# Slot attention and a feed-forward layer on one core: keys and gated values transposed by the DMA crossbar, output products between q and v, one burst of quarter-array products

## The chip, the cores and the metric

The kernel runs on one core of a Trainium2 chip. The metric is the device time of one execution in microseconds (us). A median of several executions is given, and beside it the one execution that the profiler recorded.

## The reference

Only the shapes and the data flow matter here. `x` is (2, 2048, 512) in float32.

```python
q, k, v = heads(x @ Wq, 64), heads(x @ Wk, 64), heads(x @ Wv, 128)        # 16 heads
s = clip(heads(x @ Ws, 64), -32, 32)                                      # 64 slots
z = cumlogsumexp(s, time);  p = exp(s - z);  g = exp(z_before - z)
hk = hk * g + k p^T;   ok = q hk           # per head, along time (a scan)
pv = softmax(ok)
hv = hv * g + p v^T;   ov = pv hv          # a second scan
o = rmsnorm(ov) * g_norm * silu(x @ Wg)    # gate, 128 values a head
x = layernorm(x + o @ Wo)
hidden = silu(x @ W1.T) * (x @ W3.T)       # 2048 wide
x = layernorm(x + hadamard(hidden) @ W2.T) # returned
```

The decay is carried by unnormalized exponentials: e = exp(s), a running sum z of e along time, and a division by z at the end. So both scans become masked products inside a chunk and a running state between chunks.

## The kernel before

Everything is float32. Every large product is made by Strassen's method on 2 x 2 blocks: seven block products, numbered 1 to 7, in place of eight. A product k accumulates into one of three PSUM banks, `SUM = {1: c1, 6: c1, 7: c1, 4: c1, 5: c2, 3: c2, 2: c3}`; between two products of one bank a copy of ScalarE (L462, L464) or an addition of VectorE (L467, L755) takes out what is there. A `Unit` holds these three banks; c1 has two buffers, c2 and c3 one each. The right-hand factor of a product is a tile of seven blocks: `b11, b21, b22` and four sums and differences (`right_sums`, L436 to L439).

The attention part runs over 4 groups of 4 heads (`g`) and 16 chunks of 128 positions (`n`): 64 steps. Both rows of the batch are in one step. A step has these parts:

- `load_x` (L477, or L481, L482, L485 in the first group) and `make_x` (L436 to L439, the four sums, first group alone; the finished tile is stored in DRAM, L491).
- `q`: seven products for queries, keys and slot scores (L507; order 1, 2, 5, 6, 7, 3, 4), collected in `t1`.
- `exp_s`: clamp (L515, VectorE), `e2 = exp` (L519), the old running sum added in row 0 (L520, GpSimd), `e = exp` (L521).
- `v`: seven products for values and gate (L533; order 1, then 6, 5, 2, 7, 3, 4), collected in `t2`; `tanh` (L543) and `silu` (L547) make the gate.
- products of a quarter of the array (64 x 64), two heads' halves at a time, after `v(1)`: `scores` (L589), `scores2` (L669, of the step before), `share_of_keys` (L599), `share_of_values` (L681), `slots` (L617), `values` (L692), `state_slots` (L626), `state_values` (L701). The masks `within1` (L593) and `within2` (L675) are VectorE's. This stretch is called the burst below. `running_sum` (L571, two products of the full array with a triangular matrix) stands in the middle of it.
- `reciprocal` in two halves (L582), `softmax` (L634 to L643), `softmax_sum` (L647, and L648 on GpSimd), `gated` (squares L716, products with the gate L718, sum L720, root on GpSimd L722 to L724, product L726).
- transposes: keys by four transposes of TensorE (`k_transposed`, L553, copied out at L555); gated values by eight (`o_transposed`, L743); exponentials and softmax weights by the DMA crossbar. For the crossbar each float32 is split into its two 16-bit halves by GpSimd (`e_split` L560, `r_split` L659), a DMA transposes them (L562, L661) and GpSimd joins them (`e_joined` L566, `r_joined` L665).
- `o`: seven products with Wo (L759), added to the rows (L755); `row_stats` and `normalize` in the last group; `store_rows` (L775), `load_rows` (L734).

`run(new, now, before, old)` writes out by hand the order of these parts for four steps that overlap: `now` is step i, `before` is i-1, `old` is i-2. The engines TensorE, VectorE, ScalarE and GpSimd take instructions in this order. DMAs are all issued from SyncE (SP), whose queue is in order too; where they stand in it the framework decides.

`work_on(1)` to `work_on(4)` let one piece of other work into a step, at four places (called place 1 to 4). In the first group and the beginning of the second it is `up_weights` (sums of blocks of W1 and W3 on VectorE, L784 to L787, L820 to L824; none at place 3); then `down_weights` (a product L867 at one place per step, then butterflies L891, L893); in the last group `block` (sums of the normalized rows) and `rows_transposed` (eight transposes of TensorE). In the first step of a group no piece runs; the sums of the next weights are made there and in the last step of a group (`sums`, L412 to L418).

The feed-forward part follows, with products of 256 columns (L238, L277). The change does not touch it.

The banks: `ps` are two tiles of two banks each; `flat(0)`, `bank(0)` and `bank(1)` lie in the first, scores and slots in the second.

Of the kernel before, what the change touches and what calls it, by code (L numbers as in the profile page):

```python
# [39 lines left out]
def gated_slot_attention_ffn_kernel(  # L40
# [312 lines left out]
    with ExitStack() as att:  # L353
# [87 lines left out]
        class Unit:  # L441


            def __init__(self, width, multiply):
                self.multiply, self.kept = multiply, {}
                for c in ("c1", "c2", "c3"):
                    t = pch.tile([P, 512], F32, name=c, tag=c, bufs=2 if c == "c1" else 1)
                    setattr(self, c, t[:, 0:width])

            def sum(self, k):  # L450
                return getattr(self, SUM[k])

# [16 lines left out]
        class Step:  # L469
# [79 lines left out]

            def k_transposed(self):  # L550

                for i in range(NQ):
                    nc.tensor.transpose(bank(0)[:, i, :], self.t1[:, i, P : 2 * P], ident)  # L553
                self.kr = c1.tile([P, NQ, P], F32, name="kr")
                nc.scalar.copy(self.kr, bank(0))  # L555

            def e_split(self):

                parts = c1.tile([P, 2, NQ * P], U16, name="parts")
                nc.gpsimd.tensor_copy(parts, words(self.e))  # L560
                self.et = c1.tile([P, 2 * NQ, P], U16, name="et")
                nc.sync.dma_start_transpose(out=self.et, in_=parts.rearrange("p h c -> p (h c)"))  # L562

            def e_joined(self):
                self.eT = c1.tile([P, NQ, P], F32, name="eT")
                nc.gpsimd.tensor_copy(words(self.eT), self.et.rearrange("p (h i) t -> p h (i t)", h=2))  # L566

            def running_sum(self):
                p = pch.tile([P, 512], F32, name="running", tag="c1", bufs=2).rearrange("p (i t) -> p i t", t=P)
                for j, h in enumerate(HALVES):  # L570
                    nc.tensor.matmul(p[:, :, h], lhsT=(causal, causal3[:, TH:])[j], rhs=self.e2[:, :, h], start=True, stop=True)  # L571
                z = c1.tile([P, NQ, P], F32, name="z", tag="z")
                nc.scalar.copy(z, p)  # L573
                self.z = z
                if not self.final:
                    for at, h in zip((P - 1, TH - 1), HALVES):
                        nc.sync.dma_start(out=zc[:, :, h], in_=z[at : at + 1, :, h])
                self.iz = c1.tile([P, NQ, P], F32, name="iz")
# [12 lines left out]
            def within1(self):  # L591
                self.a1 = c1.tile([P, 2, NQ, TH], F32, name="a1", tag="r")
                nc.vector.tensor_tensor(self.a1, within_scores[0], within_b, ALU.mult)  # L593

            def share_of_keys(self):

                pk = [pch.tile([P, 512], F32, name="pk", tag=f"c{2 + s}")[:, 0 : NQ * M].rearrange("p (i m) -> p i m", m=M) for s in range(2)]
                for i, j, h, s, t, _ in QUARTERS:
                    nc.tensor.matmul(pk[s][h, i], lhsT=self.kr[t, i, h], rhs=self.e[t, i, h], start=True, stop=True)  # L599

                self.hk = hk[0], hk[1], hk[2]
                hk[0], hk[2] = hk[2], hk[0]
                self.taken_in(self.hk[1], None if self.first else self.hk[0], pk[0])
                if not self.final:
                    self.taken_in(self.hk[2], self.hk[1], pk[1])

# [38 lines left out]
            def softmax_sum(self):  # L645
                self.sm = small.tile([P, NQ, 2], F32, name="sm")
                nc.vector.tensor_reduce(self.sm.rearrange("p q j -> p (q j)"), self.r8, AX.X, ALU.add)  # L647
                nc.gpsimd.tensor_tensor(self.r, self.r, self.iz, ALU.mult)  # L648

# [6 lines left out]
            def r_split(self):  # L656

                parts = c1.tile([P, 2, NQ * P], U16, name="parts_r")
                nc.gpsimd.tensor_copy(parts, words(self.r))  # L659
# [3 lines left out]
            def r_joined(self):  # L663
                self.rT = c1.tile([P, NQ, P], F32, name="rT")
                nc.gpsimd.tensor_copy(words(self.rT), self.rt.rearrange("p (h i) t -> p h (i t)", h=2))  # L665

# [10 lines left out]
            def share_of_values(self):  # L677

                pv = [bank(s) for s in range(2)]
                for i, j, h, s, t, _ in QUARTERS:  # L680
# [5 lines left out]
            def values(self):  # L686

                self.po = [
                    pch.tile([P, 512], F32, name="po", tag=f"c{2 + j}").rearrange("p (i t) -> p i t", t=DV) for j in range(2)
                ]  # L690
                for i, j, h, s, t, o in QUARTERS:
# [14 lines left out]
            def state(self):  # L706
                if not self.final:
                    self.taken_in(hv[0], hv[1], bank(1))

            def gated(self):  # L710
# [4 lines left out]
                for j, to, at in MOVES:  # L715
                    nc.scalar.activation(sq[to, j], self.po[j][at], AF.Square)  # L716
                for j, to, at in MOVES:
                    nc.vector.tensor_tensor(self.gj[to, j], self.po[j][at], self.gj[to, j], ALU.mult)  # L718
                ss = small.tile([P, 2 * NQ], F32, name="ss")
                nc.vector.tensor_reduce(ss, sq.rearrange("p j q d -> p (j q) d"), AX.X, ALU.add)  # L720
                self.state()
                nc.gpsimd.tensor_scalar(ss, ss, 1.0 / DV, 0.0, ALU.mult, ALU.add)  # L722
                nc.gpsimd.tensor_tensor(ss, ss, self.floor.rearrange("p j q -> p (j q)"), ALU.add)
# [13 lines left out]
            def o_transposed(self):  # L737
# [8 lines left out]
                self.ob = c1.tile([P, 7, 2, P], F32, name="ob")  # L746
                right_factor(self.ob, tp)

            def o(self, k):
# [261 lines left out]
        def run(new, now, before, old):  # L1011
# [36 lines left out]

            late = [nw["vg"].sums] if now is steps[0] else []
            if opens:  # L1050
                w["qks"] = nw.pop("qks")
            main("q", 1)
            do(old, "o", 3)
            work_on(1)
            if new is not steps[1]:
                do(new, "load_x")
            main("q", 2)
            do(new, "make_x")
            y["second"] = new is not None and new.g > 0
            work_on(2)  # L1060
            if changes:
                nw["vg"].sums(0, nc.vector)
            main("q", 5)
            do(before, "e_joined")
            work_on(3)
            if changes:
                nw["vg"].sums(1, nc.gpsimd)
            main("q", 6)
            do(old, "o", 6)
            do(before, "r_joined")  # L1070
            if changes:
                nw["vg"].sums(2, nc.vector)
            main("q", 7)
            work_on(4)
            if changes:
                nw["vg"].sums(3, nc.gpsimd)
            main("q", 3)
            main("q", 4)
            do(old, "o", 7)
            if last:  # L1080
                nw["qks"] = load_qks(g + 1)
            if now is steps[-1]:
                wt.append(load_w(0, 0))
                open_x("wqks", OUTER[:3], 3 * P)
            do(now, "exp_s")
            do(now, "e_split")
            do(old, "row_stats", 1)
            for f in late:
                f(0)
            if opens:  # L1090
                w["vg"] = nw.pop("vg")
            main("v", 1)
            more()
            do(before, "load_rows")
            do(now, "k_transposed")
            do(old, "o", 4)
            if o_last:
                nw["o"] = load_o(old.g + 1)

# [5 lines left out]
            do(before, "share_of_values")  # L1107
            do(now, "running_sum")
            do(old, "row_stats", 0)
            do(old, "normalize")  # L1110
            do(old, "store_rows")
            do(now, "reciprocal", 0)
            do(now, "slots")
            do(before, "values")
            do(now, "state_slots")
            do(before, "state_values")
            do(before, "gated")

            for f in late:
# [6 lines left out]
            if o_last:  # L1126
                scale_o()
            do(now, "reciprocal", 1)
            main("v", 2)
# [4 lines left out]
            if last:  # L1134
                nw["qks"].sums(0, nc.gpsimd)
                nw["qks"].sums(1, nc.gpsimd)
            if o_last:
                nw["o"].sums(0, nc.gpsimd)
                nw["o"].sums(1, nc.gpsimd)
            main("v", 7)  # L1140
            do(now, "softmax")
            main("v", 3)
            more()
            do(now, "softmax_sum")
            do(now, "r_split")
            if o_last:
                nw["o"].sums(2)
                nw["o"].sums(3, nc.gpsimd)
            do(before, "o_transposed")
            main("v", 4)  # L1150
            if last:
                nw["vg"] = load_vg(g + 1)
            do(now, "tanh")
            do(now, "squared_sums")
            if before is not None and before.first:
                w["o"] = nw.pop("o")
            do(before, "o", 1)
            do(before, "o", 5)
            more()
# [3 lines left out]
            do(now, "silu")  # L1163
            do(before, "o", 2)
            if now is steps[0]:
# [141 lines left out]
```

## Time and profile before

| what | value |
|---|---|
| median of 3 executions | 3482.67 us (3482.01 to 3483.49) |
| profiled execution, its own time | 3486.9 us |
| its span, first to last instruction | 3485.1 us |
| granted TensorE clock, mean | 0.998 |
| attention, q(1) of the first step to q(1) of the last | 9.7 to 2329.3 us |
| steps 3 to 15 apart (first group) | 35.7 to 36.9 us |
| a step with nothing beside it (1584.0 to 1619.7) | 35.7 us |
| idle of VectorE before L755, in all | 423.5 us |

In the profile PE is TensorE's matmuls, PEld its weight loads, DVE VectorE, ACT ScalarE, POOL GpSimd, SP SyncE, and SPq SyncE's DMA queue. A line of the timeline reads: start in us from the span's start, duration, engine, source line, operation, output <- input, shapes, how often; in brackets the idle time before it and what ended that. Ends of matmuls are modelled and overlap with the next start. A float32 matmul is recorded as two entries. A line of the windows gives the stretch, its length, busy time of each engine, the granted clock of TensorE, the DMA engines' share and GB/s.

### The profile page before, as it was taken

What the parts mean: (1) busy time and instruction counts of PE and PEld (TensorE: products, weight loads), DVE (VectorE), ACT (ScalarE), POOL (GpSimd) and SP (SyncE); (2) the same over time, 40 slices, a digit from 0 to 9 for tenths busy, and PEclk for the clock granted to TensorE, in tenths of its full rate; (3) what the DMA queues carried; (4) which work ended last, traced back from release to release, by engine and by line L of the source; (5) the groups of instructions that cost most, each with busy time, mean ns of one, the idle gap of its engine ahead of it and who ended that gap; (6) DMA issues with size and microseconds to landing.
All of it is one profiled execution on the core that took longest, in us unless ns stands there. A gap on an engine that the chain in (4) does not pass through costs nothing. (4 is left out here: it accounts for less than half of the span.)

```text
span 3485.1 us, 74815 instructions
## 1 busy us (share of the span) xinstructions
PE 3405.6 (98%) x31328; PEld 2664.5 (76%) x31328; DVE 2328.7 (67%) x3812; ACT 912.9 (26%) x1776; POOL 1500.0 (43%) x1389
## 2 busy tenths in 40 slices
PE   8999999999999999999999999998999999999998
PEld 6777776777777777777776777776888888888887
DVE  5777776765657756557656677777667756656756
ACT  2333332333333333333333333332111111111110
POOL 3344344433333543433444334344534634643544
PEclk9999999999999999999999999999999999999999
DMA  6545455433233433323442344467455545444441
GB/s 198 132 131 155 130 144 151 113 87 80 71 76 86 119 105 75 81 74 80 108 112 69 110 130 144 137 190 268 155 187 195 169 162 188 155 157 177 159 135 70
DMA packets 344001, 458.57 MB, mean 132 GB/s; under 512 B 154864, under 2 KB 255600, under 8 KB 342640
## 3 DMA queue, kind: packets, MB, share of 16 engines
q1 hardware_dynamic: 343664, 453.79, 43.7%
q8 instruction: 246, 4.03, 0.5%
q14 instruction: 91, 0.75, 0.1%
HBM read 297.47 MB, written 125.30 MB: 121 GB/s over the span
## 5 line engine op out<-in xcount | busy, mean ns | idle before, releaser
L533 PE MATMUL c<-wvg,xb 128*128 128x512 f32 x1792 | 811.0, 597 | 11.1 <-DVE t L718 7.3
L533 PEld LDWEIGHTS c<-wvg,xb 128*128 128x128 f32 x1792 | 321.8, 189 | 375.0 <-issue 291.7
L507 PE MATMUL c<-xb,wqks 128*128 128x128 f32 x3584 | 550.9, 276 | 26.0 <-DVE t L467 10.6
L507 PEld LDWEIGHTS c<-xb,wqks 128*128 128x128 f32 x3584 | 485.3, 193 | 49.6 <-issue 18.9
L755 DVE TENSOR_TENSOR rows<-c,rows 128x256 f32<-128x256 f32 x448 | 188.6, 422 | 423.5 <-PE c L759 423.0
L219 DVE TENSOR_TENSOR accux<-c,accux 128x512 f32<-128x512 f32 x496 | 341.3, 690 | 182.7 <-PE c L238 166.0
L277 PE MATMUL dc<-w2t,hid 128*128 128x256 f32 x1792 | 455.3, 379 | 2.1 <-DVE res L284 2.1
L238 PE MATMUL c<-wvg,xb 128*128 128x256 f32 x1792 | 433.5, 381 | 5.0 <-DVE accux L219 4.4
L238 PEld LDWEIGHTS c<-wvg,xb 128*128 128x128 f32 x1792 | 340.0, 191 | 56.2 <-DVE accux L219 7.9
L277 PEld LDWEIGHTS dc<-w2t,hid 128*128 128x128 f32 x1792 | 340.2, 190 | 49.5 <-DVE res L284 3.3
L507 PE MATMUL c<-wqks,xb 128*128 128x128 f32 x1792 | 347.9, 276 | 0.0
L238 PE MATMUL c<-wqks,xb 128*128 128x256 f32 x1344 | 326.6, 382 | 6.5 <-DVE accux L219 3.6
L462 ACT COPY kept<-c 128x384 f32<-128x384 f32 (+1 forms) x384 | 203.0, 529 | 426.9 <-PE c L507 332.5
L467 DVE TENSOR_TENSOR t<-c,kept 128x384 f32<-128x384 f32 (+1 forms) x384 | 230.0, 609 | 105.5 <-PE c L507 98.7
L238 PEld LDWEIGHTS c<-wqks,xb 128*128 128x128 f32 x1344 | 255.2, 191 | 45.6 <-DVE accux L219 6.0
L722 POOL TENSOR_SCALAR ss<-ss 128x8 f32<-128x8 f32 x64 | 12.6, 197 | 608.0 <-DVE ss L720 608.0
L507 PEld LDWEIGHTS c<-wqks,xb 128*128 128x128 f32 x1792 | 273.6, 193 | 0.0
L520 POOL TENSOR_TENSOR e<-e,zc 1x512 f32<-1x512 f32 x60 | 76.2, 1271 | 446.0 <-ACT e L519 438.1
L284 DVE TENSOR_TENSOR res<-dc,res 128x256 f32<-128x256 f32 x448 | 189.1, 423 | 117.6 <-PE dc L277 107.2
L582 DVE RECIPROCAL iz<-z 128x256 f32<-128x256 f32 x128 | 223.8, 1749 | 15.6 <-ACT z L573 15.5
L253 POOL TENSOR_TENSOR accw<-accw,accux 128x512 f32<-128x512 f32 x64 | 80.8, 1274 | 276.0 <-DVE accux L219 274.6
L718 DVE TENSOR_TENSOR t<-po,t 64x512 f32<-64x512 f32 (+1 forms) x192 | 131.5, 685 | 99.1 <-ACT sq L716 97.8
(187 smaller groups left out, 5146.8 us busy)
## 6 DMA issues: line engine op xcount, KB each, us to landing
xb<-w13s SPq DMA_DIRECT2D x112, 896.0 KB
xb<-xd SPq DMA_DIRECT2D x48, 896.0 KB
yd<-rows SPq DMA_DIRECT2D x128, 256.0 KB
w2t<-w2s SPq DMA_DIRECT2D x32, 896.0 KB
rows<-yd SPq DMA_DIRECT2D x100, 256.0 KB
xd<-xb SPq DMA_DIRECT2D x16, 896.0 KB
wvg<-fxd SPq DMA_DIRECT2D x16, 896.0 KB
w13s<-inner SPq DMA_DIRECT2D x96, 128.0 KB
```

Of the source, the lines that this page charges most:

```text
L219: nc.vector.tensor_tensor(into[:, b], s, (into if first is None else first)[:, b], ALU.add)
L238: nc.tensor.matmul(s[:, j * TQ : (j + 1) * TQ], lhsT=w[:, LEFT[k], j, :], rhs=right[:, RIGHT[k], :], start=(k in (1, 2, 5) and j == 0), st ...
L253: (nc.gpsimd if u or m == 6 else nc.vector).tensor_tensor(o, o, t["u"][:, b], ALU.add)
L277: nc.tensor.matmul(s, lhsT=h["hid"][:, i, LEFT[m], k * P : (k + 1) * P], rhs=h["w2"][:, i, RIGHT[m], :], start=(m in (1, 2, 5) and i == 0) ...
L284: nc.vector.tensor_tensor(r, s, r, ALU.add)
L462: nc.scalar.copy(self.kept[k], s)
L467: nc.vector.tensor_tensor(t[:, to], s, self.kept[other], ALU.add)
L507: nc.tensor.matmul(out[:, i * P : (i + 1) * P], lhsT=a, rhs=b, start=(k in OPENS and c == 0 and i == 0), stop=(c == 1), skip_group_check=True,
L533: nc.tensor.matmul(out, lhsT=self.xb[:, RIGHT[k], c, :], rhs=w["vg"].t[:, LEFT[k], c, :], start=(k in OPENS and c == 0), stop=(c == 1), sk ...
L582: nc.vector.reciprocal(self.iz[:, h], self.z[:, h])
L718: nc.vector.tensor_tensor(self.gj[to, j], self.po[j][at], self.gj[to, j], ALU.mult)
L755: nc.vector.tensor_tensor(y_, self.uo.sum(k), y_, ALU.add)
```

## The change

Keys and gated values take the way of the exponentials: split by GpSimd, transposed by the crossbar, joined (`k_split`, `k_joined`, `o_split`, `o_joined`, `o_sums`). All joins but half of `o_joined` move to ScalarE. All seven o products of step i-2 come between q and v of step i, in the order 1, 5, 2, then `running_sum`, then 6, 3, 7, 4. The burst has only quarter-array products. `running_sum` and the output of `values` lie in `bank(0)` and `bank(1)`, the share of values in c2 and c3, one share of keys in c1 and the other in `bank(1)`. q's order becomes 1, 5, 6, 2, 7, 3, 4. `reciprocal(1)` and the addition of the value state come earlier. Places 3 and 4 of the other work move from the q products to after `r_split` and after `silu`. The last step keeps the old way for its o products. In the diff's core lines marked "..." are left out:

```diff
 class Unit: # banks are opened at their first use
-                for c in ("c1", "c2", "c3"):
+                if c not in self.banks:
 ...
-            def k_transposed(self):
-                for i in range(NQ):
-                    nc.tensor.transpose(bank(0)[:, i, :], self.t1[:, i, P : 2 * P], ident)
+            def k_split(self):
+                keys = self.t1.bitcast(U16)[:, :, 2 * P : 4 * P].rearrange("p q (c h) -> p h q c", h=2)
+                parts = c1.tile([P, 2, NQ, P], U16, name="parts", bufs=2)
+                nc.gpsimd.tensor_copy(parts, keys)
+                self.kt = c1.tile([P, 2 * NQ, P], U16, name="kt", tag="rt")
+                nc.sync.dma_start_transpose(out=self.kt, in_=parts.rearrange("p h q c -> p (h q c)"))
+            def k_joined(self):
                 self.kr = c1.tile([P, NQ, P], F32, name="kr")
-                nc.scalar.copy(self.kr, bank(0))
+                nc.scalar.copy(words(self.kr), self.kt.rearrange("p (h i) t -> p h (i t)", h=2))
 ...
             def e_joined(self):
-                nc.gpsimd.tensor_copy(words(self.eT), self.et.rearrange("p (h i) t -> p h (i t)", h=2))
+                nc.scalar.copy(words(self.eT), self.et.rearrange("p (h i) t -> p h (i t)", h=2))
             def running_sum(self):
-                p = pch.tile([P, 512], F32, name="running", tag="c1", bufs=2).rearrange("p (i t) -> p i t", t=P)
+                p = bank(0)
 ...
+            def o_split(self):
+                gated = self.t2.bitcast(U16)[:, :, 2 * HD :].rearrange("p q (c h) -> p h q c", h=2)
+                parts = c1.tile([P, 2, NQ, HD], U16, name="parts", bufs=2)
+                nc.gpsimd.tensor_copy(parts, gated)
+                self.ot = c1.tile([P, 4 * NQ, P], U16, name="ot")
+                nc.sync.dma_start_transpose(out=self.ot, in_=parts.rearrange("p h q c -> p (h q c)"))
+            def o_joined(self):
 ...
+                nc.scalar.copy(raw[:, :, 0:2], ot[:, :, 0::2])
+                nc.gpsimd.tensor_copy(words(b12), ot[:, :, 1])
+                nc.gpsimd.tensor_copy(raw[:, :, 2], ot[:, :, 3])
+            def o_sums(self, first):
+                if first:
+                    nc.vector.tensor_tensor(ob[:, 3], b12, ob[:, 0], ALU.subtract)
+                    nc.vector.tensor_tensor(ob[:, 4], ob[:, 2], ob[:, 3], ALU.subtract)
+                else:
+                    nc.gpsimd.tensor_tensor(ob[:, 5], ob[:, 2], b12, ALU.subtract)
+                    nc.gpsimd.tensor_tensor(ob[:, 6], ob[:, 1], ob[:, 4], ALU.subtract)
 ...
 gated:
-                    nc.scalar.activation(sq[to, j], self.po[j][at], AF.Square)
+                    nc.scalar.activation(sq[to, j], self.po[j][at], AF.Square, scale=DV**-0.5)
-                self.state()
-                nc.gpsimd.tensor_scalar(ss, ss, 1.0 / DV, 0.0, ALU.mult, ALU.add)
```

The order of `run` after the change, as far as the steps i (`now`), i-1 (`before`), i-2 (`old`) and i+1 (`new`) are in the middle of the loop (`changes` and weight sums left out):

```python
now.q(1); new.load_x(); now.q(5); before.squared_sums(); new.make_x(); work_on(1)
now.q(6); old.o_joined(); now.q(2); before.r_joined(); work_on(2)
now.q(7); now.q(3); old.o_sums(True); now.q(4)
now.k_split(); now.exp_s(); old.o_sums(False)
old.o(1); old.o(5); old.o(2); now.e_split(); now.running_sum()
old.o(6); old.o(3); old.o(7); old.row_stats(1); old.o(4); old.store_rows()
now.k_joined(); now.reciprocal(0); now.open_shares(); now.v(1); before.load_rows()
now.scores(); before.scores2(); now.within1(); before.within2()
now.share_of_keys(); before.share_of_values(); now.slots(); before.values()
now.state_slots(); before.state_values()
now.reciprocal(1); old.row_stats(0); before.state(); before.gated()   # last group: then old.normalize()
now.v(6); now.v(5); now.e_joined(); now.softmax(); now.v(2); now.v(7)
before.o_split(); now.softmax_sum(); now.r_scaled(); now.r_split(); work_on(3)
now.v(3); now.v(4); now.tanh(); now.silu(); work_on(4)
```

Before, the same stretch ran:

```python
now.q(1); old.o(3); work_on(1); new.load_x(); now.q(2); new.make_x(); work_on(2)
now.q(5); before.e_joined(); work_on(3); now.q(6); old.o(6); before.r_joined()
now.q(7); work_on(4); now.q(3); now.q(4); old.o(7); now.exp_s(); now.e_split()
now.v(1); before.load_rows(); now.k_transposed(); old.o(4)
# scores to share_of_values as above; now.running_sum(); now.reciprocal(0)
# slots to state_values as above; before.gated() with the state in it
now.v(6); now.v(5); now.reciprocal(1); now.v(2); now.v(7); now.softmax(); now.v(3)
now.softmax_sum(); now.r_split(); before.o_transposed(); now.v(4); now.tanh()
before.o(1); before.o(5); now.silu(); before.o(2)
```

## The prediction

> **What bounds the kernel now.** I read the page first, then the timeline of single steps engine by engine, the waits, the DMA queue's landing records, and the built order of the changed kernel with its waits. The page:
>
> ```profile
> PE 3405.6 (98%) x31328; PEld 2664.5 (76%) x31328; DVE 2328.7 (67%) x3812; ACT 912.9 (26%) x1776; POOL 1500.0 (43%) x1389
> ```
>
> TensorE has work nearly always, so time comes off only by taking work from it, and any new wait of it is added in full. One undisturbed step (q(1) at 1584.02, next at 1619.7: 35.7 us) from the timeline of TensorE:
>
> ```profile
> 1595.99 1.88 PE L533 MATMUL c<-wvg,xb 128*128 128x512 f32 x4
> 1597.70 0.60 PE L553 MATMUL ps<-ident,t 128*128 128x128 f32 x4
> 1598.14 1.03 PE L759 MATMUL c<-wo__12005,ob 128*128 128x256 f32 x4
> ...
> 1600.08 0.65 PE L599 MATMUL pk<-e,kr 64*64 64x64 f32 x32
> 1600.55 1.05 PE L681 MATMUL ps<-t,e 64*64 64x128 f32 x32
> 1601.53 1.13 PE L571 MATMUL running<-e,causal 128*128 128x256 f32 x4
> 1602.59 0.69 PE L617 MATMUL ps<-e,a 64*64 64x64 f32 x32
> 1603.11 1.06 PE L692 MATMUL po<-t,a 64*64 64x128 f32 x32
> 1603.98 0.64 PE L626 MATMUL ps<-hk,t 64*64 64x64 f32 x32
> ...
> 1605.53 8.85 PE L533 MATMUL c<-wvg,xb 128*128 128x512 f32 x20
> 1614.48 1.09 PE L743 MATMUL ps<-ident,t 128*128 128x128 f32 x8
> 1615.41 1.88 PE L533 MATMUL c<-wvg,xb 128*128 128x512 f32 x4
> ```
>
> Starts, not durations, count: a product of v takes 1.72, of o 0.86, of q 1.34 us, the key transposes 0.44, the output transposes 0.93. VectorE is the second resource, and its queue is in order. In the first group of heads it carries the sums of the up weights too; there it already holds TensorE up, as its timeline and TensorE's show:
>
> ```profile
> 299.94 0.42 DVE L437 TENSOR_TENSOR xb<-xb,b 128x256 f32<-128x256 f32 x1
> 300.27 0.95 DVE L784 TENSOR_TENSOR inner<-both 128x256 f32<-128x256 f32 x1
> 301.14 0.94 DVE L785 TENSOR_TENSOR inner<-both 128x256 f32<-128x256 f32 x1
> 302.01 1.50 DVE L786 TENSOR_TENSOR inner<-inner,both 128x256 f32<-128x256 f32 x1
> 303.54 1.38 DVE L787 TENSOR_TENSOR inner<-both,inner 128x256 f32<-128x256 f32 x1
> ...
> 305.18 0.54 DVE L467 TENSOR_TENSOR t<-c,kept 128x384 f32<-128x384 f32 x1
> ...
> 305.78 0.71 PE L507 MATMUL c<-xb,wqks 128*128 128x128 f32 x4 [0.93 <-DVE t L467]
> ```
>
> q(4) reuses bank c1 and must wait until L467 has taken q(7) out of it; L467 stands behind a piece of weight sums. And when the loads of x go out, from the DMA queue's timeline:
>
> ```profile
> 219.15 0.36 SPq L481 DMA_DIRECT2D xb<-x_transposed  x1
> 219.57 0.41 SPq L482 DMA_DIRECT2D xb<-x_transposed  x1
> 221.42 1.28 SPq L661 DMA_TRANSPOSE rt<-parts_r  x1
> ```
>
> **What TensorE is spared, per step.** Key transposes 0.44. Output transposes 0.93, and the wait before them, 0.26 (the last v matmul starts at 1613.79, takes 0.43, and L743 starts at 1614.48, when POOL's L726 is done). The running sum leaves the burst: share_of_values and running take 2.04 (1600.55 to 1602.59); values, of the same shape, takes 0.87, and running alone among full-array work 0.86, as an o product of the same columns: 0.31 less. Sum 1.94; times 63 steps, 122 us.
>
> **What it newly waits for, per step.** Three round trips lose their cover.
> - Running now follows q(4) with only o(1), o(5), o(2) between, 2.59. Its chain from the end of q(4): 0.20 to ScalarE, copy 0.48 (L464), 0.05, clamp 0.42 (L515), 0.09, exp 0.63 (L519), 0.08, GpSimd's addition of the old sum 1.27 (L520), 0.05: 3.27. Wait 0.68, plus 0.06 for a first weight load that nothing hides: 0.74. k_split, a copy like L560 (1.03), goes ahead of L520 and just fits in; at L665's longest (2.34) it would cost 1.0 more.
> - o(4) follows o(7) into the same bank: 0.20, L755 0.42, 0.05, 0.06: 0.73. Before, products of q lay between.
> - slots waits for the mask L675, which ends 2.59 after scores starts; without running in between TensorE is there at 2.32. With the semaphore and the first load 0.37.
>
> Sum 1.84: the whole saving but 0.1 us is returned. I take 5 us gained over the steps that have nothing else, with ±0.5 us per step as bounds (the 1.0 of k_split in half of them; the 0.37 of slots absent).
>
> Sums at no cost: the joins on ScalarE (about 1.06 each, as tanh L543 on 1024 columns) and the splits on GpSimd lie beside v and q. They wait for the crossbar: o_split ends 11.3 us after the burst (squares 1.95, three L718, L720 at 5.2, L723 to L726 at 9.2, a copy twice L560's), and o_joined is due by 17.7, with r_joined behind it ahead of q(4)'s copy at 20.0. rt and et, half as large, landed 3.45 and 4.32 us (medians) after the issue began, 1.24 to 1.28 of it issue. For ot I take one more issue time, 5 us, lands 16.4: hidden. The bounds are 3.5 and twice et, 8.6; the latter lands at 20.0 and costs 2.1 in each step that has no other wait, some 100 us. VectorE's page of the Trainium skill ("VectorE: DVE Perf Modes", section "The three transpose paths") speaks against this move: it gives a 128x128 bf16 transpose as 390 ns on TensorE and 1309 ns through the crossbar, and advises TensorE where PSUM will do; for 16 blocks in a row that would be an estimate of 21 us and would break the cover altogether, but rt and et landed 8 blocks in 3.45 and 4.32, so I don't use it.
>
> **Where it loses: the first group.** No o product lies between v(4) and q now, so q(4) is due 18.46 us after the burst (v 10.41, six q products 8.05) instead of about 24, while VectorE still has ahead of q(7)'s L467: silu (ends 13.5), the piece of place 4, moved here, make_x, place 1, q(2)'s L467, place 2. Moreover the transposes are queued on SP ahead of the next x: ot, rt, then L481 and L482 (built order). r_split ends at 13.75, rt's issue at 15.1, x is issued at 15.15 and 15.55 and lands 2.79 and 2.93 later (medians): make_x's L437 ends at 18.9, though everything behind it was ready. Then, alternating: place 1 1.46, L467 0.5, place 2 4.3 (its four rows here 4.58, the means of L784 to L787 on such shapes 4.1), L467 0.5: 25.6, a wait of 7.1; or 1.33, 0.5, 2.9, 0.5: 24.1, a wait of 5.7. Before, these steps took 36.9 and 35.7, with about 1.1 and 0 of such waits: 5.95 more per step in 12 steps, 71 us. Two steps without pieces 1.5 each, 3. Four steps in the second group, without make_x, 1.9 each, 8. Eight butterfly steps of the down weights (L891, L893: three pieces at 1.5 before q(7)'s L467) 0.9 each, 7. Three changes of group, where GpSimd's weight sums stand ahead of o_split, 3 each, 9. Bounds of the first group's term: zero gain is excluded by the row of 0.93 above; half if VectorE's pieces run at their shortest and x lands early, 36; a fifth more, 85.
>
> After a wait as long, the clock. A row of windows shows it after an idle of 1.98 us (waiting for L467 at 1776.87):
>
> ```profile
> 1777.00:1781.00 4.00, 4.00 (x17) 3.77 (x18) 0.28 (x1) 0.48 (x1) 1.78 (x1) 0.57 0.03 10
> ```
>
> The granted clock was halved for 3.4 us; that is 1.7 of work, of which the wait before running takes back some: 1.5 in 12 steps, 18. Bounds 0 (two starts 1.78 apart at 601 us, with q's 0.11 usual, showed no drop) and two such stretches, 36. "TensorE: Matmul & The Clock Gate" (What's actually happening) has the rule: half speed after an idle window of about 3.4 us; by it a wait of 5.7 to 7.1 always pays. The row dropped after less.
>
> **Sum.** -5 + 71 + 3 + 8 + 7 + 9 + 18 = 111. The profiled execution took 3486.9 (span 3485.1 and 1.8 around it), 4.2 over the median 3482.67; so 3598 there, 3594 as a median.
>
> **Rivals.** (1) ot lands late (twice et): ScalarE, in order, then delays q(4)'s copy and exp in the later groups too: 100 more, 3694. For it: SP issues four transposes a step, one of double size; against: landings of rt at 3.45 leave 1.5 us of room. (2) Faster: the pinch is absent, because SP sends x off before rt, and the three round trips overlap with VectorE's and GpSimd's slack: at best 122 less, 3361; with half returned 3422. It decides if the chain of 3.27 fits under 2.59 and make_x starts by 15. Against: the rows above add up past both. (3) No change: round trips as reckoned but VectorE clears the pieces in time: 3478.
>
> **How the numbers follow.** Forecast 0.64, rival 1 0.2, rival 2 0.1, rival 3 0.06, of which half within 0.2% (7 us, about what a measurement of this kernel tells from no change) and the other half just above it. Faster 0.1, same 0.03, slower 0.87. The range: from 3594 down by 30 (0.5 in 60 steps), 36 (first group) and 18 (clock), 3510; up by 90 towards rival 1, 3685.
>
> **What will tell.** Right: steps of the first group 42 to 45 us apart, TensorE's longest waits being on L467's successor, in runs of 5 to 7, VectorE idle before L436 on a DMA; steps of the second and third groups 35.5 to 36.7 as before; small waits of TensorE on the GpSimd addition and on the rows' addition, about 0.7 each, some 60 times; granted clock below 0.998. Wrong: ScalarE waiting on ot in every step (rival 1), or steps near 34 (rival 2).

## The result and the profile after

The changed kernel took 3727.43 us (median of 4 runs, 3723.87 to 3728.9) beside 3483.08 us for the kernel before on the same chip: ratio 1.07, 95% interval 1.0682 to 1.0719. The forecast had the direction right (slower) and the size wrong: 111 us were reckoned, 244 came, and the time lies 42 us above the top of the range.

The first line of the page is TensorE's, and below it are its longest waits: engine, line, what it waited for, then us in all, times, the longest.

```profile
PE 3392.6 (91%) x30504; PEld 2641.5 (71%) x30504; DVE 2360.8 (63%) x3752; ACT 1184.7 (32%) x1901; POOL 1669.6 (45%) x1510
```

```profile
PE c L508 <- DVE t L468: 150.8, 38, 8.1
PE ps L577 <- POOL e L521: 36.3, 49, 3.1
PE c L801 <- DVE rows L797: 35.9, 59, 0.6
```

TensorE is busy for 13 us less than before and idle for 252 us more (spans 3724.3 and 3485.1). The granted clock is 0.976 in the mean, against 0.998, and products at half clock count as busy for longer, so the 13 us are not the whole of the products saved. The first wait is q(4) held by VectorE; the second and third are the round trips at the running sum and at o(4) that the prediction named, at 0.74 and 0.61 us each in the mean (0.74 and 0.73 foretold).

The distance from each step's q(1) to the next, after minus before, says where the 239 us of span lie:

| Stretch | after − before, us | the prediction's terms |
|---|---|---|
| steps 3 to 14, first group | +101.2 | 71 + 18 |
| nine steps at the group changes (15, 16, 18, 31, 32, 34, 47, 48, 50) | +58.8 | 9 |
| the other steps from 17 to 49 | +26.1 | 3 + 8 + 7 |
| steps 51 to 62, last group | +30.2 | none |
| last q(1) to the end | +17.0 | none |
| steps 0 to 2, and ahead of them | +6.0 | none |
| round trips against products saved, all steps | 0.07 in a plain step | −5 in all |

The first group, from the timeline of the changed kernel (start, duration, engine, line; in brackets the idle time before and who ended it):

```profile
341.66 1.76 SPq L769 DMA_TRANSPOSE ot<-parts  x1
344.87 1.24 SPq L677 DMA_TRANSPOSE rt<-parts  x1
346.21 0.88 SPq L482 DMA_DIRECT2D xb<-x_transposed  x1
...
349.62 0.43 DVE L436 TENSOR_TENSOR xb<-b,xb 128x256 f32<-128x256 f32 x1 [3.37 <-DMA xb<-x_transposed]
...
355.63 1.02 DVE L468 TENSOR_TENSOR t<-c,kept 128x384 f32<-128x384 f32 x2
...
356.24 1.22 PE L508 MATMUL c<-xb,wqks 128*128 128x128 f32 x4 [7.22 <-DVE t L468]
```

The x load goes out behind the transposes of ot and rt; VectorE stands still for 3.37 us at L436 with two pieces and both of q's additions queued behind it; q(4) starts 7.22 us late. In seven of the twelve steps the wait at L436 ended with this load; in the other five (2.9 to 3.4 us) the profile names a product or nothing. The table of windows (us, PE busy, PEld, DVE, ACT, POOL, the granted clock, DMA share, GB/s) shows the clock around that wait:

```profile
349.00:356.00 7.00, 0.02 (x1) 0.00 (x0) 6.31 (x12) 1.35 (x2) 3.35 (x4) 0.69 0.82 278
356.00:363.00 7.00, 6.76 (x25) 6.05 (x26) 2.68 (x7) 1.74 (x3) 3.26 (x4) 0.58 0.47 131
```

A step next to a group change (18; 34 and 50 look the same), VectorE's and GpSimd's rows of the timeline:

```profile
781.96 0.68 DVE L661 TENSOR_REDUCE sm<-r 128x8 f32<-128x512 f32 x1
782.85 1.89 POOL L767 COPY parts<-t 128x2048 uint16<-128x2048 uint16 x1
...
786.02 1.04 POOL L675 COPY parts<-r 128x1024 uint16<-128x1024 uint16 x1
787.02 1.26 POOL L412 TENSOR_TENSOR wo__6370<-low,wo__6370 128x512 f32<-128x512 f32 x1
788.31 1.73 DVE L416 TENSOR_TENSOR wo__6370<-wo__6370 128x512 f32<-128x512 f32 x1 [5.68 <-POOL wo__6370 L412]
```

GpSimd's first sum of the o weights now stands behind o_split and r_split; VectorE waits 5.68 us for it, ahead of v(3)'s addition; the next q(4) then waits 5.3 us. In steps 16, 32 and 48 VectorE waits for the weights of v and gate instead (5.7, 9.0 and 10.2 us), whose loads stand behind ot and rt on SyncE (in step 32 the loads L407 went out at 1327.46, the second of these transposes at 1325.79):

```profile
1333.82 1.23 DVE L412 TENSOR_TENSOR wvg<-low,wvg 128x1024 f32<-128x1024 f32 x1 [8.96 <-DMA wvg<-wvg_blocks]
```

In these three steps TensorE waits twice, first for GpSimd's sums of the q, k, s weights (L418) and then for VectorE; in step 16:

```profile
705.54 0.71 PE L508 MATMUL c<-xb,wqks 128*128 128x128 f32 x4 [2.72 <-POOL wqks L418]
715.63 1.23 PE L508 MATMUL c<-xb,wqks 128*128 128x128 f32 x4 [8.08 <-DVE t L468]
```

And a step of the last group, where piece 3 (L833 to L836) now lies beside GpSimd's copies:

```profile
2262.74 0.41 DVE L833 TENSOR_TENSOR halves<-yq 128x256 f32<-128x256 f32 x1
2263.07 2.11 DVE L834 TENSOR_TENSOR halves<-yq 128x256 f32<-128x256 f32 x1
2264.87 1.44 POOL L664 TENSOR_TENSOR r<-r,iz 128x512 f32<-128x512 f32 x1
...
2267.69 0.68 DVE L468 TENSOR_TENSOR t<-c,kept 128x512 f32<-128x512 f32 x1
```

The addition L834 takes 0.42 us among the q products, and 2.11 here beside o_split, which ran from 2262.85 to 2264.91; v(3)'s addition L468 comes late and the next step's q(5) waits 1.9 us.

### The profile page after: what moved, and what is told of

It is laid out like the page before. It is cut to its first block, busy times and chain, and to the rows that moved or that the text cites. A ratio compares the mean times of both kernels' runs of the same rounds, so it can differ in the third digit from the quotient of the medians.

```text
span 3724.3 us, 73698 instructions
## 1 busy us (share of the span) xinstructions
PE 3392.6 (91%) x30504; PEld 2641.5 (71%) x30504; DVE 2360.8 (63%) x3752; ACT 1184.7 (32%) x1901; POOL 1669.6 (45%) x1510
## 4 chain that ended last, share of the span: by engine, by line
PE 69%; DVE 12%; POOL 6%; issue 6%; DMA 4%; ACT 2%; SPq 1%; POOLq 0%; DVEq 0%; ACTq 0%
PE c L238 17%; PE c L534 14%; PE c L508 10%; PE dc L277 10%; PE c L801 8%; PE ps L577 2%; PE ps L717 2%; POOL e L521 2%; DVE t L468 2%; PE ps L708 2%; POOL parts L555 1%; ACT sq L732 1%; PE ps L631 1%; DVE a L599 1%; DVE t L734 1%
## 5 line engine op out<-in xcount | busy, mean ns | idle before, releaser
L534 PE MATMUL c<-wvg,xb 128*128 128x512 f32 x1792 | 804.0, 599 | 14.8 <-DVE t L468 14.0
L508 PE MATMUL c<-xb,wqks 128*128 128x128 f32 x3584 | 578.7, 286 | 177.5 <-DVE t L468 150.8
L508 PEld LDWEIGHTS c<-xb,wqks 128*128 128x128 f32 x3584 | 501.4, 201 | 219.8 <-DVE t L468 158.7
L534 PEld LDWEIGHTS c<-wvg,xb 128*128 128x128 f32 x1792 | 330.9, 190 | 407.7 <-issue 349.0
L238 PEld LDWEIGHTS c<-wvg,xb 128*128 128x128 f32 x1792 | 338.9, 190 | 55.8 <-DVE accux L219 9.0
L508 PE MATMUL c<-wqks,xb 128*128 128x128 f32 x1792 | 359.9, 284 | 0.0
L468 DVE TENSOR_TENSOR t<-c,kept 128x384 f32<-128x384 f32 (+1 forms) x384 | 229.4, 617 | 131.5 <-PE c L508 128.4
L238 PEld LDWEIGHTS c<-wqks,xb 128*128 128x128 f32 x1344 | 256.2, 192 | 47.6 <-DVE accux L219 7.9
L508 PEld LDWEIGHTS c<-wqks,xb 128*128 128x128 f32 x1792 | 285.3, 201 | 0.0
L619 POOL TENSOR_TENSOR hk<-hk,kept 128x256 f32<-128x256 f32 x60 | 44.8, 746 | 423.5 <-DVE hk L625 392.9
L737 POOL TENSOR_TENSOR ss<-ss,floor 128x8 f32<-128x8 f32 x64 | 16.5, 258 | 482.4 <-DVE ss L736 482.4
L555 POOL COPY parts<-t 128x1024 uint16<-128x1024 uint16 x64 | 82.9, 1295 | 276.0 <-ACT t L465 236.1
```

Source lines behind the costliest of these rows:

```text
L238: nc.tensor.matmul(s[:, j * TQ : (j + 1) * TQ], lhsT=w[:, LEFT[k], j, :], rhs=right[:, RIGHT[k], :], start=(k in (1, 2, 5) and j == 0), st ...
L468: nc.vector.tensor_tensor(t[:, to], s, self.kept[other], ALU.add)
L508: nc.tensor.matmul(out[:, i * P : (i + 1) * P], lhsT=a, rhs=b, start=(k in OPENS and c == 0 and i == 0), stop=(c == 1), skip_group_check=True,
L534: nc.tensor.matmul(out, lhsT=self.xb[:, RIGHT[k], c, :], rhs=w["vg"].t[:, LEFT[k], c, :], start=(k in OPENS and c == 0), stop=(c == 1), sk ...
L555: nc.gpsimd.tensor_copy(parts, keys)
```

## The experiments

Theory: the products are a fair exchange in a plain step; the loss is made by in-order queues (SyncE's loads, GpSimd's weight sums, VectorE's x sums and pieces) that the new order put ahead of what q and v wait for. Rivals: the crossbar and its joins are late in every step; the halved clock alone; VectorE is simply full. All times below are medians; the table after the eighth run splits them by stretch.

**The x loads on another queue.**

```diff
-  nc.sync.dma_start(out=self.xb[...], in_=src[...])     # L482, L483, L486, first group
+  nc.scalar.dma_start(out=self.xb[...], in_=src[...])
```

> The changed kernel with one edit: the three x loads of the first group (L482, L483, L486) go out on ScalarE's queue instead of SyncE's, where they stand behind the transposes of the gated outputs and of r. Everything is computed as in the changed kernel (3727.4 us). Theory (the order of SyncE's queue makes the first group slow: VectorE sits idle 3.4 us before L436 for x and TensorE then waits 7.2 us at q(4)): x lands some 4 us earlier, the wait falls by about 3.4 us in each of 12 steps, 41 us less: 3686 us; if the half clock after the wait goes as well, 1.7 to 3.4 us a step more: 3645 to 3665 us. Rival A (VectorE's pieces or GpSimd's copies set the wait, x would only be next): under 10 us, 3718 to 3730 us, and VectorE's idle time before L436 turns into a wait for something else. Rival B (the o products between q and v cost the time by themselves, in every step alike): no change.

3715.08 us, ratio 1.0662 (1.0646 to 1.0678). The first group lost 14.7 of its 101.2 us, not 41. The loads of xb went out 4 us sooner in the step (1.6 us behind q(1) instead of 5.4), yet VectorE still waited, for the other load, b:

```profile
339.14 0.96 ACTq L486 DMA_DIRECT2D b<-x_transposed  x1
...
345.31 0.43 DVE L436 TENSOR_TENSOR xb<-b,xb 128x256 f32<-128x256 f32 x1 [3.14 <-DMA b<-x_transposed]
```

The run does not tell the theories apart as meant. On SyncE, whose order is not fixed by hand, b is loaded about two steps ahead (its last load goes out at 528.7 us there, at 601.1 here); on ScalarE it goes out in its own step, and its use came 6.2 us behind its issue, beside ot, rt and stores of weights. So the run shows that an earlier xb is worth something; how much it doesn't show.

**The pieces back among the q products.**

```diff
-  work_on(3) after r_split; work_on(4) after silu
+  work_on(2) after q(6); work_on(3) after q(2); work_on(4) after q(7)
```

> The changed kernel with VectorE's pieces of other work put back near where the kernel before had them: piece 2 after q(6), piece 3 after q(2), piece 4 after q(7), none after r_split or after silu. Everything is computed. Theory (in the first group it is SyncE's queue that holds x, in the last group it is the pieces at places 3 and 4 that hold VectorE's v sums back so that the next q(5) and q(4) wait): first group about the same or up to 2 us a step slower, as the pieces now stand between the sums that q(4) needs (0 to +24 us); steps 54 to 62 faster by 1.5 to 2.5 us each, 15 to 20 us less; together 3705 to 3735 us. Rival A (the piece at place 4 makes the first group slow): 12 steps by 5 to 7 us, 3640 to 3670 us. Rival B (neither): 3727 us with no change in either group.

3727.42 us, no change in the sum. The first group stayed at +102.8, and VectorE's wait for x only grew (25.6 to 56.7 us from 170 to 650 us): the piece at place 4 is not its cause. Steps 56 to 61 lost 11 of their 20 us and step 47 lost 8, as the theory has it; steps 33, 54 and 62 gave 17 back (in step 54 the piece itself waited 6.4 us for its load, with the o sums behind it).

**TensorE kept working through the wait.**

```diff
   main("q", 3)
+  if g == 0 and now.n > 2: seven 128x512 products into ps[0][:, 1]
   main("q", 4)
```

> The changed kernel with seven more matrix products (128x512, into a bank that nothing reads then) ahead of q(4) in steps 3 to 15 of the first group, so that TensorE works through most of its 7 us wait there instead of sitting idle; their results are not used and the output stays the same. Theory (the idle wait drops the granted clock to one half for some 6.8 us in each step, which makes q(4) and the o products 3.4 us longer): the half-clock stretches of the first group go, 12 times 3.4 us less, 41 us: 3686 us. Rival A (what follows the wait is set by VectorE's or GpSimd's chain and not by TensorE's own time): the clock stays full but the steps stay at 44 us: 3720 to 3730 us. Rival B (the waits are shorter than the seven products in most steps): longer by 1 us a step, 3740 us.

3725.69 us, ratio 1.0703 (1.0687 to 1.072), so the 41 us did not come. The seven products took 6.17 us and the wait behind them 1.39; the same two windows now read

```profile
349.00:356.00 7.00, 5.61 (x24) 3.30 (x23) 6.07 (x12) 0.39 (x1) 2.29 (x3) 1.00 0.86 287
356.00:363.00 7.00, 5.88 (x27) 4.46 (x25) 2.91 (x7) 3.26 (x5) 4.87 (x5) 1.00 0.77 232
```

with the clock full throughout. The first group fell by 17.4 us (101.2 to 83.8), 1.45 a step: the halved clock is worth about that, and most of the rest is the wait. The other steps were 15 us longer in this profile; 5.8 of that are stalls in the burst that come up again below, the rest is not explained.

**Weight loads and sums on other engines.**

```diff
-  wvg loads on nc.sync;  nw["qks"].sums(1, nc.gpsimd)
+  wvg loads on nc.scalar;  nw["qks"].sums(1)
```

> The changed kernel with two edits at the three group changes: the loads of the next group's v and gate weights go out on ScalarE's queue instead of SyncE's, and the second sum of the next q, k, s weights is made by VectorE instead of GpSimd. Everything is computed. Theory (each group change costs some 18 us more than before because SyncE's weight loads stand behind the transposes and GpSimd's weight sums stand ahead of the copies that feed them): steps 16, 32 and 48 lose 6 to 10 of their 12 us, 18 to 30 us in all: 3697 to 3709 us. Rival A (the weight sums on VectorE just move the wait to q's own sums): 0 to 10 us, 3717 to 3727 us. Rival B (the loads are slow because of the slot they wait for, not of the queue): 3725 us and ScalarE now waits with its copies behind the loads, up to +15 us.

3724.51 us. Steps 32 and 48 lost 7.0 and 3.5 us, step 16 only 0.5, and steps 15, 31 and 47 gave 8.5 back, so that the nine steps stayed at +56.5. In step 16 the loads now go out at 701.75, ahead of rt's transpose instead of behind it, and the issue of rt, 1.24 us otherwise, took

```profile
704.03 5.67 SPq L677 DMA_TRANSPOSE rt<-parts  x1
```

VectorE still waited 8.6 us for the last of these loads (5.7 before this edit), so their place on SyncE's queue is not the whole reason why they come late. TensorE's wait for GpSimd's L418 in steps 16, 32 and 48 fell from 8.5 us together to 0.9. The next runs leave the loads and move their consumers back.

**The x sums behind the o products.**

```diff
-  main("q", 5); squared_sums; do(new, "make_x")
+  ... do(now, "reciprocal", 0); do(new, "make_x")
```

> The changed kernel with one edit: the sums of the next step's x (L436 and L437 on VectorE, L438 and L439 on GpSimd, and the store of x) stand behind the o products, after the reciprocals, instead of after q(5). Everything is computed. In the run with the x loads on ScalarE's queue, VectorE still sat idle 2.3 us a step before L436, because a load can't be issued before the last product of the step before has freed its tile. Theory (in the first group VectorE waits in order at L436 for x, and the addition that q(4) needs stands behind it; the pieces and the half clock come after that): the wait at q(4) falls from 7 us to under 2 us, the first group's steps fall from 44 to 45 us to about 38, 70 to 80 us less: 3647 to 3657 us. Rival A (VectorE has too little time in these steps whatever the order): the wait comes back at v or at the scores, 20 us less at most: 3707 us. Rival B (the o products or GpSimd's copies set the step): no change.

3643.7 us, ratio 1.0462 (1.0447 to 1.0478): 84 us less by one moved line. The first group fell to +20.5, and no other stretch moved by more than 2.3. So four fifths of the first group's loss is the place of the x sums.

**The weight sums later.**

```diff
-  o.sums(2), o.sums(3) after r_split; vg.sums(0..3) among q(5) to q(7); qks.sums(0, 1) ahead of o_split
+  o.sums(2), o.sums(3) after silu;   vg.sums(0..3) ahead of v(1);     qks.sums(0, 1) ahead of gated
```

> The changed kernel with the weight sums of the three group changes moved and nothing else: the last two sums of the o weights after silu (VectorE's sits idle 5.7 us for GpSimd's first one ahead of a v sum in steps 18, 34 and 50), the four sums of the v and gate weights ahead of v(1) instead of between the q products (VectorE sits idle 5.7 to 9 us for their loads in steps 16, 32 and 48), and the first two sums of the q, k, s weights ahead of the gate instead of ahead of o_split. Everything is computed. Theory (in-order queues hold the sums that the next product needs): of the 57 us that steps 16, 18, 32, 34, 47, 48 and 50 lost against the kernel before, 35 to 45 go: 3682 to 3692 us. Rival (the copies and transposes of the change are late in these steps by themselves): under 15 us: 3712 to 3727 us.

3688.79 us, ratio 1.0597 (1.0581 to 1.0612): the nine steps fell from +58.8 to +15.3. Step 18 stayed at +6.7: VectorE still waits 2.2 us for GpSimd there, in the new place. Step 47 stayed at +7.1 too: there a piece of the down weights (L941) waits 4.7 us for its load ahead of q's additions, and moving the pieces takes it away (the second run above, the tenth below).

**Two products moved.**

```diff
-  e_split; running_sum; o(6); o(3); o(7); o(4); v(1)
+  e_split; o(6); running_sum; o(3); o(7); v(1); o(4)
```

> The changed kernel with two products moved and nothing else: the running sum after o(6) instead of before it, and o(4) after v(1) instead of before it. Everything is computed. Theory (the round trips that the burst brought are real and cost each step: 0.55 us at the running sum, 53 times, and 0.61 us at o(4), 59 times): 60 to 65 us less where the steps have nothing else that waits, less in the first group; ordinary steps of groups 2 and 3 at 35.5 us instead of 36.6: 3660 to 3690 us. Rival (VectorE's additions of the rows and the c banks set the pace, so the wait only moves to the keys' product or to the next v): under 20 us: 3707 to 3727 us.

3633.77 us, ratio 1.043 (1.0413 to 1.0448): 94 us less, more than the theory or the rival had. Two rows of TensorE's timeline of a plain step (25) in the changed kernel, and in this run:

```profile
1067.87 1.13 PE L577 MATMUL ps<-e,causal 128*128 128x256 f32 x4 [0.56 <-POOL e L521]
...
1072.20 1.10 PE L801 MATMUL c<-wo__6370,ob 128*128 128x256 f32 x4 [0.61 <-DVE rows L797]
```

```profile
1037.87 3.62 PE L801 MATMUL c<-wo__6365,ob 128*128 128x256 f32 x16
1041.33 1.03 PE L577 MATMUL ps<-e,causal 128*128 128x256 f32 x4
```

Neither wait is left, and the step took 34.96 us against 36.63 after and 36.56 before. So the exchange is 1.6 us a step in the change's favour once these two round trips are covered. (The third, slots behind its mask, stays: from the share of values to slots TensorE takes 1.20 us, where values, of the same shape, takes 0.87.) Of the 1.67 regained, 1.17 are the two waits; TensorE's busy time fell by 0.43 too (35.29 to 34.86). Of that, 0.17 is the longer first product behind a wait (1.13 and 1.10 above against 1.03); the rest may be the modelled ends, which overlap the next start only where no wait lies between. In such a step no matmul waits for the crossbar either.

**The three together.**

> The three edits together: the x sums behind the o products, the weight sums of the group changes moved, the running sum after o(6) and o(4) after v(1). Everything is computed. Theory: the three gains add, 70 to 80, 35 to 45 and 40 to 65 us: 3540 to 3580 us, still above the 3482.9 us of the kernel before, by the last group and the tail. Rival (the waits cover each other, or VectorE is the next bound): less than 120 us in all: over 3607 us.

3498.26 us, ratio 1.0038 (1.0025 to 1.0052): 229 us less; the three alone gave 84, 39 and 94, together 216. The gains add, and a little more than that: the 3540 to 3580 expected were too high. After minus before by stretch, us of span:

| Run | 3 to 14 | group changes | others 17 to 49 | 51 to 62 | end |
|---|---|---|---|---|---|
| the change | 101.2 | 58.8 | 26.1 | 30.2 | 17.0 |
| TensorE kept working | 83.8 | 66.2 | 37.9 | 27.8 | 11.9 |
| x sums later | 20.5 | 56.6 | 27.7 | 30.1 | 17.9 |
| weight sums later | 103.0 | 15.3 | 31.5 | 31.1 | 14.8 |
| two products moved | 93.3 | 47.9 | −26.5 | 12.4 | 16.4 |
| all three | 4.2 | 2.0 | −25.5 | 13.3 | 13.2 |
| and pieces 3 and 4 (below) | 2.8 | −15.4 | −21.8 | 1.6 | 18.8 |

**Piece 3 away from GpSimd's copies.**

```diff
-  work_on(3) after r_split; o.sums(2), o.sums(3) after silu
+  work_on(2) after q(6); work_on(3) after q(2); o.sums(2), o.sums(3) after o_sums(True), a step later
```

> The three edits together (as in the run before, 3498.3 us) and two more: piece 3 goes back among the q products (piece 2 after q(6), piece 3 after q(2); piece 4 stays after silu), and the last two sums of the next o weights stand behind the first sums of the o products, one step later. Everything is computed. In the run before, the four additions of a piece at place 3 (128x256) took 0.42, 2.11, 1.48 and 1.14 us beside GpSimd's scaling and copy of r, against 0.42 us each among the q products, and the v sum behind them came 3.6 us late in steps 56, 57, 58, 61 and 62. Theory (that collision holds the v sum that the next q(5) needs, and the clock halves after it): steps 54 to 62 lose 15 us, steps 18 and 34 lose 8 us, the tail 3 to 5 us: 3470 to 3476 us, below the 3482.6 us of the kernel before. Rival (VectorE is full in the last group, so the additions delay q(4) instead): no more than 8 us less, by steps 18 and 34 alone: 3490 to 3498 us.

3494.62 us, ratio 1.0035 (1.0022 to 1.0048): not the 3470 to 3476 expected. The mechanism shows (steps 54 to 61 lost 9.7 us; piece 3's additions take 0.41, 0.92, 0.92 and 0.42 us now), but step 62, steps 43 to 45 and the first group gave 15 us back.

**Piece 4 as well.**

```diff
-  work_on(4) after silu
+  work_on(4) after q(7); one more empty place ahead of a block's first additions
```

> As the run with piece 3 among the q products, with piece 4 moved too, from behind silu to behind q(7), where the kernel before had it, and with one more empty place between the loads of a block and its first additions. Everything is computed. Theory (place 3 is what collided; place 4 stands beside the o copies of GpSimd or beside nothing, and its move trades a wait at q(4) against one at the o products): within 8 us of the run with piece 3 alone, either way. Rival (piece 4 ahead of q's sums is a second cause of the same kind): another 10 to 15 us less, 3458 to 3465 us, with the steps of the first group below 36 us.

3470.38 us, ratio 0.9963 (0.995 to 0.9976): 24 us below the run before it, the rival's side and more, and 0.4% below the kernel before. The run has two edits, and nothing tells them apart; the first group's steps (35.6 to 39.4 us) did not all fall below 36. It has the change's new ways for keys and gated values and its place for the o products. Pieces 3 and 4 are back among the q products, so that part of the change is undone; the x sums, the weight sums, the running sum and o(4) stand in other places than in the change. In eight of its steps TensorE waits for the keys, whose copy L561 waits for kt from the crossbar, 13.5 us together.

**The running sum later still.**

```diff
-  o(6); running_sum; o(3); o(7)
+  o(6); o(3); running_sum; o(7)      # next run: o(6); o(3); o(7); running_sum
```

> As the run with pieces 3 and 4 among the q products (3470.4 us), with the running sum one product later: after o(3) instead of o(6). Everything is computed. There TensorE still waited at the running sum for GpSimd's addition of the carried row, 20.9 us in 32 times (0.65 us each). Theory (that wait is the last round trip of the burst that stands in the open; one more product of 0.9 us covers it): 12 to 20 us less: 3450 to 3458 us. Rival (the copy of z, the reciprocals and the keys' product come later with it, and the wait moves there): under 5 us, 3465 to 3473 us.

3472.97 us, ratio 0.9968 (0.9955 to 0.998): no gain. The wait at the running sum (20.9 us in 32 times) was nearly gone (3.4 in 2), and stalls in the burst of quarter-array products grew from 14.7 to 31.4 us: waits that the profile puts down to "issue", that is to nothing it shows. The kernel before has 6.4 us of these, the change 26.2, the run with the extra products 32.0. What makes them was not tried and stays open.

> As the run with the running sum after o(3), one product later still: after o(7), right ahead of v(1). Everything is computed. Theory (the wait is covered already after o(3), and from there each product later only moves the copy of z and the copy of the transposed keys behind it): 0 to 6 us more than the run with it after o(3), with waits at the keys' product for ScalarE's copy of the keys. Rival (the wait at the running sum is longer than one product in many steps): 3 to 8 us less than that run.

3487.63 us, ratio 1.0014 (1.0005 to 1.0023): 15 us more than the run before it, against 0 to 6 expected. In that run the running sum stood right ahead of o(7), whose factor GpSimd makes at L788. Without this cover o(7) waits for it, 13.0 us in 28 times; what makes the rest of the 15 was not followed:

```profile
PE c L801 <- POOL ob L788: 13.0, 28, 1.7
```

## Why the prediction was right and wrong

**Right: the exchange in a plain step.** 1.94 saved against 1.84 returned was foretold; a plain step took 36.63 us against 36.56. The waits were of the size foretold: counted between starts, 0.74 us at the running sum, 0.78 at o(4) and 0.32 at slots, against 0.74, 0.73 and 0.37. With the first two covered the step fell by 1.67.

**Right: the first group's mechanism.** Waits of 7.1 and 5.7 in turn were worked out; the trace has 7.07 to 7.87 in the even steps and 5.41 to 6.88 in the odd ones, x behind rt on SyncE included. Over the twelve steps these waits grew from 5.6 to 79.2 us, by 74 where 71 was reckoned. (5.95 a step is a small slip: 7.1, 5.7 and 1.1 make 5.85.) The term was 89 with the clock and measured 101.2; moving make_x alone took off 80.7. The clock's 18 was 17.4, which is luck: the half clock lasted 6.8 us in most of these steps and not 3.4, and more than half of what it took did not show in the time, presumably because other waits hid it.

**Wrong: "Three changes of group, where GpSimd's weight sums stand ahead of o_split, 3 each, 9".** This term was mis-sized, and it is the step that did most to put the time outside the range: 58.8 measured, of which 43.5 went when the sums alone were moved. I saw one queue and priced one wait. A wait of that size is there, though not by way of o_split: TensorE stood 2.7, 3.4 and 2.5 us for GpSimd's L418 itself in steps 16, 32 and 48. What I left out cost more. The loads of v's and gate's weights go out behind ot and rt on SyncE, VectorE waits 5.7 to 10.2 us for them among the q products, and TensorE then 8.1, 6.8 and 6.7 us at q. GpSimd's o sums moved behind r_split, VectorE's L416 waits 5.7 us for them ahead of a v addition in each of steps 18, 34 and 50, and TensorE then 5.3. In step 47 a piece that waits for its load costs TensorE 6.2. And half clock followed each of these. The move of the o sums past v(7), o_split and r_split stands in the diff; I didn't follow it, and it hits the step two after the change of group, where I didn't look.

**Wrong: nothing for the last group and the end, 47 us together.** I costed pieces 3 and 4 in the first group alone. In the last group piece 3 costs because of what lies beside it: 0.42 us became 2.11 next to o_split, and TensorE then waits 1.9 us at q(5) in each of steps 56, 57, 58, 61 and 62. Moving the pieces took 11 of the 20 us of steps 56 to 61; of the rest of the 30.2, the share of each wait was not separated. The end was not tested by itself: the last o product comes 98.5 us after the last q(1) against 79.9 before, and it stayed so in the fastest run (98.7). That no q or v follows there to cover the burst's round trips is a guess.

**Too low: the remaining steps of groups two and three,** 18 reckoned and 26.1 measured, and not by the waits that I reckoned. The waits at q(4) make 10.9 us in all of these steps (1.0 to 1.8 in each of the butterfly steps 29, 30 and 43 to 46, where I had 0.9). Stalls in the burst that the profile puts down to nothing grew from 2.3 to 13.6 us there; their cause stays open.

**Rival 1 lay nearest in time (3694) and is wrong.** Its mechanism, ot twice as late, did not occur: in the DMA queue's landing records ot took 4.32 us (median of 63), inside the 5 that I took. ScalarE's copy L777 did wait for ot in 38 steps, 43 us together, but in a plain step it didn't, and q(4)'s copy there waited for TensorE and not the reverse. The crossbar rule of "VectorE: DVE Perf Modes" (The three transpose paths), 1309 ns a transpose, doesn't fit these 16 blocks in 4.32 us either.

## What to carry to other kernels

When a step is moved, list for each in-order queue what now stands ahead of the instructions that the bottleneck waits for, in the steps that have other work beside them (first group, group changes, last group) as well as the plain one: here the exchange in a plain step was a wash, and those others made most of the loss. A load that can't go out sooner is best met by moving its consumer back: one moved line gave 84 us here, another queue for the load 12. And where products are the cover of a round trip, moving one uncovers another: look at what the moved product itself covered.

## What the runs showed that I had not expected

- VectorE's additions with two operands in SBUF ended with the GpSimd instruction beside them in step 56: L834 started at 2263.07 and ended at 2265.18, o_split ran from 2262.85 to 2264.91. "SBUF — State Buffer" (SBUF: two separate sides) tells of one shared port pair, held for a whole instruction; the rows agree.
- ScalarE's copy of 1024 uint16 columns for a join took 1.34 us where I took 1.06 from tanh on 1024 float columns.
- The half clock mostly lasted twice as long as the one stretch that I had read in the kernel before, 6.8 us and not 3.4. A short wait can be enough: in step 56 one of 1.94 us ended at 2268.43; the four matmuls right behind it took 0.71 us, those from 2270.86 on 1.22 and 1.06, where 0.61 is usual.
